# A gated decoder on one core: the conditional expert blocks behind everything, and the last attention head turned by TensorE

## The chip, the cores and the metric

The kernel runs on one core of one Trainium2 chip. The core has five engines with a queue of instructions each: TensorE (PE in the profile; its weight loads are PEld), VectorE (DVE), ScalarE (ACT), GpSimd (POOL) and SyncE (SP), which issues most DMAs. An engine takes its own instructions in order and waits on semaphores for the others. The metric is the device time of one execution in microseconds (us), as the median of several runs.

## The reference

Four layers are added to x (4 sequences of 512 tokens, 512 wide), each with a gate tanh(g). Each layer works on the layer norm of x.

```python
x = x + tanh(g_xattn[0]) * L0_xattn(layernorm(x), ctx, ...)   # x mixed by softmax(q k^T), d = 128
x = x + tanh(g_ffn[0])   * L0_ffn(layernorm(x), ...)          # a 512x512 linear with weights from bits
x = x + tanh(g_xattn[1]) * L1_xattn(layernorm(x), ctx, ...)   # 16 heads of 128, q and k normed
x = x + tanh(g_ffn[1])   * L1_ffn(layernorm(x), ...)          # 16 experts of 352, top 4
```

The third layer, per sequence and head:

```python
q = rmsnorm(h @ Wq, gq); k = rmsnorm(ctx @ Wk, gk); v = ctx @ Wv
attn = softmax(q @ k.T * 128 ** -0.5)
out = concat_heads(attn @ v) @ Wo
```

The fourth layer, for the tokens of the first sequence (the table of choices covers 512 tokens):

```python
out[token] += weight * (silu(xs @ gate[e].T) * (xs @ up[e].T)) @ down[e].T   # for each of 4 chosen e
```

## The kernel before

Everything is float32. A 128x512 float32 matmul is two passes in the trace, so its records come in pairs. x stays in SBUF as x_sb, one tile of 128 tokens by 512 for each of 16 token blocks.

**Stages.** The first layer, then the linear layer and the routing (`route`) run first; the first score matmul of the third layer starts at 211 us. The rest is the third layer with the expert blocks of the fourth spread through it. There are 32 groups m (4 sequences by 8 pairs of heads), and 64 heads i = 2m + h. The work is written out by hand as 64 steps of one head each, and two more; a step has four quarters, one for each chunk of 128 queries. `step(i)` lists what each quarter holds, `put` adds the expert work and the layer norms, and inside `manual_schedule` each engine gets its instructions in the order in which they are written. `later(n, f)` puts f off until a counter, which `tick` advances with the matmuls, has moved on by n.

**One head.** `scores(i, c)` multiplies a chunk of 128 queries with 512 keys into psS (L709). DVE takes the maximum (L717, L719), ACT the exponential with its row sum (L722), DVE the reciprocal and the scaling (L726, L727). The probabilities must be turned so that keys lie on the partitions. `turn_probs` (L243) transposes blocks of 32 by 32 on DVE into tP, and after the fourth chunk `move_probs` (L251) puts the blocks in place with 16 DMAs on SP's queue (tP to big). Two steps later `values(i)` multiplies v with them into psO (L749), ACT copies the result to oT (L756), and `project(m, chunks)` multiplies oT with Wo into psA (L776); DVE adds it to x_sb (L258). After the last group of a sequence the rows of x_sb go out (L771). In even steps the keys and values of the next group are made (L586), in odd steps its queries (L660). The keys are normed, turned on DVE and written to DRAM and read back by DMAs from ACT's queue (L630, L638).

**Psum.** Tags and buffers: psA 3, psS 2, psT 2, psO 1. A matmul into a buffer waits until the reader of what lay there is done.

**Experts.** Each expert takes up to 128 tokens as one slot; slots 16 and up are for experts with more. Slot 16 and the 16 regular ones are always worked, one in two steps, from step 22 (`block_work`): rows are gathered (`load_rows`), transposed (L845), multiplied (L853, L881), and the result goes to the table y_d in DRAM (`keep_rows`, L890). Step 56 is the last of them (`last`). At its end `count_over` loads the number of extra slots into a register of every engine (L932).

**The conditional.** Between step 56 and step 57 stands `further(17)` (L894): if more than one extra slot is in use, it works slot 17, and in it, nested, all further ones up to 30. With the inputs here the number is 1, so every engine skips the body. [...] the skip path of each engine waits for that engine's own earlier work and adds the difference.

Then steps 57 to 60 fetch four rows of y_d each per token from POOL's queue (`add_row`, L915) and add them to x_sb, weighted, and the remaining heads follow. Steps 64 and 65 hold only the values of heads 62 and 63 and their projections.

Of the kernel before, what the change touches and what calls it, by code (L numbers as in the profile page):

```python
# [15 lines left out]
P = 128  # L16
NB = 4
S = 512
DM = 512
# [35 lines left out]
def tile_gated_decoder(  # L55
# [31 lines left out]
    def ps_a():  # L87
        return ps("psA", 3)
# [443 lines left out]
    turned, moved = {}, {}  # L532

    def cols(m):
        g = groups[m][1]
# [19 lines left out]


    clock, pending, serial = [0], [], iter(range(1 << 30))
    quiet = [False]

    def later(n, f):  # L560
        heapq.heappush(pending, (clock[0] + n, next(serial), f))

    def tick(n=1):
        if n == 0:
            return
        clock[0] += n
        while pending and pending[0][0] <= clock[0]:
            heapq.heappop(pending)[2]()
# [135 lines left out]
    def scores(i, c):  # L704


        m, h = divmod(i, G)
        sc = ps_s()
        nc.tensor.matmul(  # L709
            sc, q_of[m][h][:, c * P : (c + 1) * P], k_of[m][:, :, h, :], start=True, stop=True  # L710
        )
# [24 lines left out]
        tick()  # L736
        later(0, top)
        later(2, share)
        later(3, turn)

    def values(i):
# [18 lines left out]

        later(0, copy)

    def project(m, chunks):

        b, g = groups[m]
        oT, wo = o_of[m], wo_of[m]

        def add(t, pp):
            add_to_x(t, pp, tg[:, 1:2])
            if g == NG - 1 and b > 0:  # L770
                nc.sync.dma_start(out_v[:, t, :], x_sb[:, t, :])  # L771

        for c in chunks:
            pp = ps_a()
            for j in range(G):
                nc.tensor.matmul(  # L776
                    pp, oT[:, j, c * P : (c + 1) * P], wo[:, j, :], start=(j == 0), stop=(j == G - 1)
                )
                tick()
            later(1, lambda t=b * NC + c, pp=pp: add(t, pp))  # L780
# [68 lines left out]
    def hidden(st, a):  # L849

        st[a] = ps_a()
        for k in range(KC):
            nc.tensor.matmul(  # L853
                st[a][:, :FF], st["xgT"][:, k * P : (k + 1) * P], st["gu"][:, a, k, :],
                start=(k == 0), stop=(k == KC - 1),
            )
            tick(0 if quiet[0] else 0.7)


    def gate(st):  # L860
# [17 lines left out]
    def down(st):  # L878
        st["py"] = ps_a()
        for f, (_, n) in enumerate(FCH):  # L880
# [4 lines left out]
            tick(0 if quiet[0] else 1)  # L885

    def keep_rows(s, st):
        y = row("y", 2)
        nc.vector.tensor_copy(y, st["py"])
        nc.sync.dma_start(y_d[s * P : (s + 1) * P, :], y)  # L890

    def further(s):

        with tc.If(n_over[0] > s - NE):  # L894
            quiet[0] = True
            load_hidden(s)
            load_down(s)
            load_rows(s)
# [5 lines left out]
            gated(st)  # L904
            hidden_T(st)
            down(st)
            keep_rows(s, st)
            quiet[0] = False
            if s + 1 < NSLOT:
                further(s + 1)  # L910

    def add_row(c, k):

        yg = row("y", 2)
        nc.gpsimd.indirect_dma_start(  # L915
            out=yg,
            out_offset=None,
            in_=y_d[:, :],
            in_offset=bass.IndirectOffsetOnAxis(ap=posi[:, k, c : c + 1], axis=0),
        )  # L920

        def add():
            add_to_x(c, yg, tw[:, c * TOPK + k : c * TOPK + k + 1])
# [10 lines left out]
    def block_work(s, then):  # L934
# [8 lines left out]
            (1, 2): [lambda: down(st()), lambda: later(1, lambda: keep_rows(s, st()))],  # L943
        }
        if then is not None:
            work_of[0, 3] = [lambda: load_hidden(then)]
# [79 lines left out]
    def step(i):  # L1026
        m, h = divmod(i, G)
        pieces = [[], [], [], []]
        if i >= G:
            pieces[2].append(lambda: values(i - G))  # L1030
        elif h > 0:
            pieces[3].append(lambda: tick(8))
        if h == 0:
            if 0 < m < M - 1:
                pieces[0].append(lambda: keys_values(m + 1, [0, 1]))
# [7 lines left out]
        else:  # L1043
            if m + 1 < M:
                pieces[0].append(lambda: queries(m + 1, 0))
                pieces[1].append(lambda: queries(m + 1, 1))
# [85 lines left out]
```

## Time and profile before

Three runs took 1504.64, 1505.93 and 1507.05 us. The profiled execution took 1506.07; its span, from the first instruction to the last, is 1504.3.

| | us |
|---|---|
| median of 3 runs | 1505.93 |
| profiled execution | 1506.07 |
| its span | 1504.3 |
| PE busy (with PEld beside it: 671.2) | 1440.6 |
| DVE busy | 961.6 |
| ACT busy | 522.1 |
| POOL busy | 287.4 |
| the 16 DMA engines, share held by SP's and ACT's queues | 40.8% and 7.3% of the span |

A row of the costliest groups names line, engine, operation, tiles out<-in, shape and count; then the busy time and the mean of one in ns; then the idle time of the engine just before these instructions and what ended most of it. Matmuls are pipelined, so the mean of one is latency; what one costs in a row of them is the distance from start to start. A row in order of time has start, duration, engine, line, tiles and count, and in brackets the idle time before it with its releaser. A row of stretches has the stretch, its length, the busy time (and count) of PE, PEld, DVE, ACT and POOL, the granted PE clock (1.00 is full), the share of the DMA engines and GB/s.

### The profile page before, as it was taken

To read this page: it belongs to the slowest core of one execution; us is meant where nothing else is said; L and a number is where in the kernel's file an instruction comes from. 1 tells how busy PE (TensorE), PEld (TensorE's weight loads), DVE (VectorE), ACT (ScalarE), POOL (GpSimd) and SP (SyncE) were. 2 spreads that over 40 slices of the span, in tenths; PEclk is the share of its full clock that TensorE was granted. 3 is DMA by queue.
4 is the path that set the end of the run, shared out by engine and by line. 5 is a ranking of instruction groups with operands and counts; after the bars stand their busy time and mean duration, and the time that the engine had idled before them with its cause. 6 is when DMAs were issued, how large, how long until landed. Compare 5 with 4: busy or idle time off the path is not lost. (4 is left out here: it accounts for less than half of the span.)

```text
span 1504.3 us, 13711 instructions
## 1 busy us (share of the span) xinstructions
PE 1440.6 (96%) x3705; PEld 671.2 (45%) x3705; DVE 961.6 (64%) x2170; ACT 522.1 (35%) x1175; POOL 287.4 (19%) x210
## 2 busy tenths in 40 slices
PE   5899999899999999999999999999999999989987
PEld 2444444344444444444444444444444444434433
DVE  5875537577777777666565655566656655666783
ACT  3521224333343433333333333324333333333331
POOL 2434411221111111111101111112011111112210
PEclk8899999999999999999999999999999999999998
DMA  9610013554444546456665665556656655545643
GB/s 332 231 47 1 15 56 84 151 145 135 126 143 135 147 137 178 117 170 193 174 185 171 184 203 155 174 163 201 184 164 184 184 169 177 171 121 156 182 126 91
DMA packets 156114, 227.93 MB, mean 152 GB/s; under 512 B 24832, under 2 KB 90896, under 8 KB 156032
## 3 DMA queue, kind: packets, MB, share of 16 engines
q1 hardware_dynamic: 128080, 178.91, 40.8%
q10 hardware_dynamic: 23040, 33.56, 7.3%
q0 software_dynamic: 4912, 14.53, 3.4%
q8 instruction: 32, 0.52, 0.1%
q14 instruction: 50, 0.41, 0.1%
HBM read 129.62 MB, written 30.17 MB: 106 GB/s over the span
## 5 line engine op out<-in xcount | busy, mean ns | idle before, releaser
L722 ACT ACTIVATE prob<-psS,sb,rq 128x512 f32<-128x512 f32 x256 | 199.2, 778 | 605.3 <-DVE sb L719 582.0
L709 PE MATMUL psS<-kT,qT 128*128 128x512 f32 x512 | 263.1, 597 | 4.5 <-DMA big<-tP 2.5
L776 PE MATMUL psA<-wo,oT 128*128 128x512 f32 x512 | 238.6, 604 | 11.7 <-ACT oT L756 11.7
L660 PE MATMUL psA<-lnT,wq 128*128 128x512 f32 x512 | 232.9, 596 | 8.2 <-DVEq L894 7.6
L749 PE MATMUL psO<-big,v 128*128 128x512 f32 x512 | 232.8, 598 | 5.2 <-DMA big<-tP 5.2
L586 PE MATMUL psA<-wkv,ctx 128*128 128x512 f32 x512 | 233.5, 596 | 0.2 <-DVE x_sb L258 0.2
L717 DVE TENSOR_REDUCE nmax<-psS 128x1 f32<-128x512 f32 x256 | 173.0, 676 | 39.5 <-PE psS L709 37.6
L243 DVE STREAM_TRANSPOSE tP<-prob 128x512 f32<-128x512 f32 x256 | 181.9, 711 | 9.0 <-DVE prob L727 0.6
L726 DVE RECIPROCAL rden<-den 128x1 f32<-128x1 f32 x256 | 40.6, 159 | 224.6 <-ACT prob L722 219.0
L749 PEld LDWEIGHTS psO<-big,v 128*128 128x128 f32 x512 | 98.1, 192 | 129.6 <-issue 121.7
L776 PEld LDWEIGHTS psA<-wo,oT 128*128 128x128 f32 x512 | 96.9, 193 | 131.0 <-issue 105.4
L660 PEld LDWEIGHTS psA<-lnT,wq 128*128 128x128 f32 x512 | 97.2, 191 | 129.6 <-issue 107.6
L173 POOL TENSOR_TENSOR rq<-qss,mhalf 128x8 f32<-128x8 f32 x32 | 53.3, 1667 | 516.6 <-DVE qss L696 516.6
L258 DVE SCALAR_TENSOR_TENSOR x_sb<-psA,tg,x_sb 128x512 f32<-128x512 f32 x160 | 113.8, 728 | 57.6 <-PE psA L776 21.8
L586 PEld LDWEIGHTS psA<-wkv,ctx 128*128 128x128 f32 x512 | 96.8, 191 | 118.8 <-issue 106.5
L727 DVE TENSOR_SCALAR prob<-prob,rden 128x512 f32<-128x512 f32 x256 | 133.5, 521 | 9.0
L173 POOL TENSOR_TENSOR rk<-kss,mhalf 128x8 f32<-128x8 f32 x32 | 52.5, 1640 | 447.5 <-DVE rden L726 279.8
L709 PEld LDWEIGHTS psS<-kT,qT 128*128 128x128 f32 x512 | 93.2, 191 | 95.6 <-issue 73.2
L853 PE MATMUL psA<-gu,xgT 128*128 128x352 f32 x272 | 86.0, 459 | 0.0
L623 DVE STREAM_TRANSPOSE tK<-kn 128x256 f32<-128x256 f32 x128 | 45.5, 413 | 49.5 <-POOL kn L612 49.5
L853 PEld LDWEIGHTS psA<-gu,xgT 128*128 128x128 f32 x272 | 51.7, 190 | 37.9 <-issue 16.3
L756 ACT COPY oT<-psO 128x512 f32<-128x512 f32 x64 | 37.4, 585 | 77.4 <-PE psO L749 70.2
(157 smaller groups left out, 1283.7 us busy)
## 6 DMA issues: line engine op xcount, KB each, us to landing
big<-tP SPq DMA_DIRECT2D x1024, 64.0 KB
wq<-in_wq_dram SPq DMA_DIRECT2D x32, 512.0 KB
wo<-in_wo_dram SPq DMA_DIRECT2D x32, 512.0 KB
k_d<-tK ACTq DMA_DIRECT2D x32, 512.0 KB
kT<-k_d ACTq DMA_DIRECT2D x128, 128.0 KB
gu<-in_gate_dram SPq DMA_DIRECT2D x16, 704.0 KB
gu<-in_up_dram SPq DMA_DIRECT2D x16, 704.0 KB
wkv<-in_wk_dram SPq DMA_DIRECT2D x32, 256.0 KB
```

Of the source, the lines that this page charges most:

```text
L173: nc.gpsimd.tensor_tensor(out, v, mhalf[:, :n], ALU.pow)
L243: nc.vector.transpose(tP[:, :, c, :], e.rearrange("p (j r) -> p j r", r=TB))
L258: nc.vector.scalar_tensor_tensor(x_sb[:, t, :], src, gate, x_sb[:, t, :], ALU.mult, ALU.add)
L586: nc.tensor.matmul(pp, ctxs[b][:, k, c * P : (c + 1) * P], wkv[:, k, :, :].rearrange("p a n -> p (a n)"), start=(k == 0), stop=(k == CC - 1),)
L660: nc.tensor.matmul(pp, wq[:, k, h * D : (h + 1) * D], lx1[b][:, k, :], start=(k == 0), stop=(k == KC - 1))
L709: nc.tensor.matmul(sc, q_of[m][h][:, c * P : (c + 1) * P], k_of[m][:, :, h, :], start=True, stop=True)
L717: nc.vector.tensor_reduce(nmax, sc, AX.X, ALU.max, negate=True)
L722: nc.scalar.activation(st["e"], sc, AF.Exp, bias=sb, scale=scale, accum_out=st["den"])
L727: nc.vector.tensor_scalar(st["e"], st["e"], rden, None, ALU.mult)
L749: nc.tensor.matmul(po, v[:, k, h * D : (h + 1) * D], pT[:, :, k, :], start=(k == 0), stop=(k == NC - 1))
L776: nc.tensor.matmul(pp, oT[:, j, c * P : (c + 1) * P], wo[:, j, :], start=(j == 0), stop=(j == G - 1))
L853: nc.tensor.matmul(st[a][:, :FF], st["xgT"][:, k * P : (k + 1) * P], st["gu"][:, a, k, :], start=(k == 0), stop=(k == KC - 1),)
```

## The change

1. The conditional blocks leave their place between steps 56 and 57. All steps now stand in one stretch, and a new function `spill` follows them. In its body, which runs if more than one extra slot is in use, a second table more_d is filled with zeros, `further(17)` writes its slots there, and 16 gathers add the rows to x_sb once more and store the first sequence's rows again. `add_row` keeps reading y_d, where slots 17 to 30 are zero.
2. `project` takes psA, psO, psT and psA for chunks 0, 1, 2 and 3, in every group.
3. The last head (63) has no 32x32 transposes and no moves. Its exponential writes the columns in another order; `end_turn(c)` transposes four 128x128 pieces of chunk c on PE and copies them (DVE for even c, ACT for odd), and `end_values(c)` multiplies v with the 128 queries of that chunk and copies them to oT.
4. Step 63 is the last. It holds values(61) in its first quarter, the projection of group 30 in quarters 2 and 3, and in the last quarter values(62), the pieces of head 63 and the projection of group 31 chunk by chunk. Steps 64 and 65 are gone.

In the built program the last output store stands on SP behind the conditional; the three before it stand ahead of it. The load of wo at the end of step 56 stands behind the moves of head 56, not ahead of them.

```diff
@@ route and tables
+    more_d = dram.tile([NSLOT * P, DM], F32, name="more_d")
...
@@ scores
-            nc.scalar.activation(st["e"], sc, AF.Exp, bias=sb, scale=scale, accum_out=st["den"])
+            e, x = st["e"], sc
+            if i == n_heads - 1:
+                e = e.rearrange("p (k t r) -> p k t r", k=NC, r=TB)
+                x = sc.rearrange("p (t k r) -> p k t r", t=NT, r=TB)
+            nc.scalar.activation(e, x, AF.Exp, bias=sb, scale=scale, accum_out=st["den"])
...
         def turn():
+            if i == n_heads - 1:
+                ends[c] = st["e"]
+                return
...
+    def end_turn(c):
+        if c == 0:
+            ends["pT"] = big()
+        e, pt = ends.pop(c), ps_t()
+        for k in range(NC):
+            nc.tensor.transpose(pt[:, k * P : (k + 1) * P], e[:, k * P : (k + 1) * P], ident)
+        tick(0.5)
+        dst = ends["pT"][:, :, c * P : (c + 1) * P]
+        copy = nc.scalar.copy if c % 2 else nc.vector.tensor_copy
+        later(0, lambda: copy(dst, pt.rearrange("p (k q) -> p k q", k=NC)))
+
+    def end_values(c):
+        m, h = divmod(n_heads - 1, G)
+        po = ps_a()
+        for k in range(NC):
+            nc.tensor.matmul(
+                po[:, 0:P], v_of[m][:, k, h * D : (h + 1) * D],
+                ends["pT"][:, k, c * P : (c + 1) * P], start=(k == 0), stop=(k == NC - 1),
+            )
+        tick(1)
+        later(0, lambda: nc.scalar.copy(o_of[m][:, h, c * P : (c + 1) * P], po[:, 0:P]))
...
@@ project
-            pp = ps_a()
+            pp = (ps_a, ps_o, ps_t, ps_a)[c]()
...
+    def spill():
+
+        with tc.If(n_over[0] > SPILL):
+            zero = row("xgT", 1)
+            nc.vector.memset(zero, 0.0)
+            nc.sync.dma_start(
+                more_d.rearrange("(s p) d -> p s d", p=P),
+                zero.unsqueeze(1).broadcast_to([P, NSLOT, DM]),
+            )
+            further(NE + SPILL)
+            for c in range(NC):
+                for k in range(TOPK):
+                    add_to_x(c, rows_of(more_d, c, k), tw[:, c * TOPK + k : c * TOPK + k + 1])
+                nc.sync.dma_start(out_v[:, c, :], x_sb[:, c, :])
...
@@ step
         if i >= G:
-            pieces[2].append(lambda: values(i - G))
+            pieces[0 if i == n - 1 else 2].append(lambda: values(i - G))
...
+        if i == n - 1:
+            pieces[1].append(lambda: project(m - 1, [0, 1]))
+            pieces[2] += [lambda: project(m - 1, [2, 3]), lambda: end_turn(0)]
+            pieces[3] += [lambda: values(i - 1), lambda: end_turn(1)]
+            pieces[3] += [lambda: end_values(0), lambda: end_turn(2), lambda: end_values(1)]
+            pieces[3] += [lambda: project(m, [0]), lambda: end_turn(3), lambda: end_values(2)]
+            pieces[3] += [lambda: project(m, [1]), lambda: end_values(3)]
+            pieces[3] += [lambda: project(m, [2]), lambda: project(m, [3])]
...
     with tc.manual_schedule():
-        for i in range(last + 1):
-            step(i)
-    further(NE + SPILL)
-    with tc.manual_schedule():
-        for i in range(last + 1, n + G):
+        for i in range(n):
             step(i)
         tick(20)
+    spill()
```

More of the change, by code (lines that the diff above doesn't have):

```diff
@@ L531, in tile_gated_decoder @@
     q_of, sq_of, rq_of, kn_of, k_of, v_of, o_of = {}, {}, {}, {}, {}, {}, {}
-    turned, moved = {}, {}
+    turned, moved, ends = {}, {}, {}
+    n_heads = G * len(groups)
     def cols(m):
@@ L557, in tile_gated_decoder @@
     clock, pending, serial = [0], [], iter(range(1 << 30))
-    quiet = [False]
     def later(n, f):
@@ L563, in tick @@
     def tick(n=1):
-        if n == 0:
-            return
         clock[0] += n
@@ L856, in hidden @@
             )
-            tick(0 if quiet[0] else 0.7)
+            tick(0.7)
     def gate(st):
@@ L884, in down, with keep_rows @@
             )
-            tick(0 if quiet[0] else 1)
-    def keep_rows(s, st):
+            tick()
+    def keep_rows(s, st, table):
         y = row("y", 2)
         nc.vector.tensor_copy(y, st["py"])
-        nc.sync.dma_start(y_d[s * P : (s + 1) * P, :], y)
+        nc.sync.dma_start(table[s * P : (s + 1) * P, :], y)
     def further(s):
         with tc.If(n_over[0] > s - NE):
-            quiet[0] = True
             load_hidden(s)
@@ L906, in further, with rows_of @@
             down(st)
-            keep_rows(s, st)
-            quiet[0] = False
+            keep_rows(s, st, more_d)
             if s + 1 < NSLOT:
                 further(s + 1)
-    def add_row(c, k):
+    def spill():
[11 more added lines that the diff above has]
+                nc.sync.dma_start(out_v[:, c, :], x_sb[:, c, :])
+    def rows_of(table, c, k):
         yg = row("y", 2)
@@ L917, in add_row @@
             out_offset=None,
-            in_=y_d[:, :],
+            in_=table[:, :],
             in_offset=bass.IndirectOffsetOnAxis(ap=posi[:, k, c : c + 1], axis=0),
         )
+        return yg
+    def add_row(c, k):
+        yg = rows_of(y_d, c, k)
         def add():
@@ L942, in block_work @@
             (1, 0): [lambda: hidden_T(st())],
-            (1, 2): [lambda: down(st()), lambda: later(1, lambda: keep_rows(s, st()))],
+            (1, 2): [lambda: down(st()), lambda: later(1, lambda: keep_rows(s, st(), y_d))],
         }
@@ L1042, in step @@
                 pieces[3].append(lambda: later(4, lambda: load_wo(m)))
-        else:
+        elif i < n - 1:
             if m + 1 < M:
```

## The prediction

> **What bounds the kernel now.** I read the page's first part, then its costliest groups, then TensorE (PE) in order of time in the last 165 us, then that stretch with all engines. Times below are us from the span's start.
>
> ```profile
> span 1504.3 us, 13711 instructions
> PE 1440.6 (96%) x3705; PEld 671.2 (45%) x3705; DVE 961.6 (64%) x2170; ACT 522.1 (35%) x1175; POOL 287.4 (19%) x210
> ...
> L776 PE MATMUL psA<-wo,oT 128*128 128x512 f32 x512 | 238.6, 604 | 11.7 <-ACT oT L756 11.7
> L660 PE MATMUL psA<-lnT,wq 128*128 128x512 f32 x512 | 232.9, 596 | 8.2 <-DVEq L894 7.6
> L749 PE MATMUL psO<-big,v 128*128 128x512 f32 x512 | 232.8, 598 | 5.2 <-DMA big<-tP 5.2
> ```
>
> PE is the bound: 96% busy, 63.7 us idle in the whole span, and in the middle steps nearly nothing to gain: between 570 and 1345 the order of time shows no idle worth a mark before any PE group. A change in the tail is therefore worth the PE idle that it removes and the PE work that it adds. Two idle stretches lie where the change works. L894 is the conditional: 7.6 us before L660. L749 waits 5.2 us for the moved probabilities of the last head.
>
> ```profile
> 1347.38 1.02 PE L709 MATMUL psS<-kT,qT 128*128 128x512 f32 x2
> 1356.00 5.33 PE L660 MATMUL psA<-lnT,wq 128*128 128x512 f32 x8 [7.60 <-DVEq L894]
> 1361.16 1.02 PE L709 MATMUL psS<-kT,qT 128*128 128x512 f32 x2
> 1362.02 3.60 PE L660 MATMUL psA<-lnT,wq 128*128 128x512 f32 x8
> ...
> 1408.81 1.13 PE L776 MATMUL psA<-wo,oT 128*128 128x512 f32 x2 [2.63 <-ACT oT L756]
> ...
> 1446.86 1.12 PE L776 MATMUL psA<-wo,oT 128*128 128x512 f32 x2 [1.80 <-ACT oT L756]
> ...
> 1463.23 1.88 PE L709 MATMUL psS<-kT,qT 128*128 128x512 f32 x4
> 1466.41 1.12 PE L709 MATMUL psS<-kT,qT 128*128 128x512 f32 x2 [1.30 <-DMA big<-tP]
> ...
> 1487.33 6.20 PE L749 MATMUL psO<-big,v 128*128 128x512 f32 x8 [5.21 <-DMA big<-tP]
> 1493.37 7.11 PE L776 MATMUL psA<-wo,oT 128*128 128x512 f32 x16
> ```
>
> Columns: start, duration, engine, line, tiles, count, idle before and its releaser. The reader is to see three things. The same eight matmuls take 5.33 after the 7.60 idle and 3.60 six us later; after the 5.21 idle they take 6.20. And the granted clock, by stretches (start:end, length, PE, PEld, DVE, ACT, POOL busy, then the clock), says why:
>
> ```profile
> 1356.00:1361.00 5.00, 5.00 (x8) 2.27 (x9) 0.00 (x0) 0.00 (x0) 0.00 (x0) 0.67 0.45 112
> 1361.00:1400.00 39.00, 39.00 (x93) 17.32 (x92) 28.72 (x60) 14.55 (x33) 13.09 (x11) 1.00 0.53 146
> ...
> 1448.00:1450.00 2.00, 2.00 (x5) 0.97 (x5) 0.99 (x4) 0.87 (x2) 0.00 (x0) 0.51 0.48 182
> ```
>
> So a pause costs its length and then matmuls at half clock. The last row follows an idle of only 1.80 us, while the 2.63 idle at 1408.81 was followed by a full clock: a short pause may or may not cost it.
>
> **Part 1, the conditional leaves step 57.** Its body doesn't run: 4 gathers of gate weights and 17 y_d stores are those of the 17 unconditional slots. What stalls PE is L660: its psum buffer would have been last read inside the body, so it waits for a DVE count that the skip path gives only when DVE reaches the branch, after all its softmax work (branch at 1355.3). POOL's row gathers likewise wait for SP's skip path (1363.0). Without it PE goes on at 1348.4, when the score matmul before ends. Gain: 7.60 idle + (5.33 - 3.60) slow restart = 9.3. The register load of the count stays (0.5 to 0.9 us on each engine's queue); PE's was done at 1342.3 while matmuls were queued, so nothing. On SP the wo load now goes behind sixteen probability moves and that register load, some 14 us later (1347.6 to about 1361.5); its reader, project of the group, comes at 1405, so nothing.
>
> What the pause covered: ACT and DVE caught up in it. In the next two steps with the same work, PE then waits for ACT's oT copy (2.63, 1.80), since ACT stood at the key reloads (L638). I walked step 57 without the pause: PE reaches project's second matmul at 1348.4 + 3.43 + 0.86 + 3.43 + 0.86 + 3.43 + 0.86 + 0.86 = 1362.1; ACT's oT copy ends at about 1361.8 if the four key reloads take some 2 us (0.80 + 0.93 at 1363.2), and at about 1363.9 if 4 us, as at 1402.4. So 0 to 2.6 of new idle, and up to 1.7 of half clock behind it: from 0 to 4.3. I take 1.0, near the quick reload. Net 8.3.
>
> **Part 2, project's psum.** Chunks 1 and 2 of every project move from psA (3 buffers) to psO (1) and psT (2). The PE work is the same. The next user of psO, values, comes two quarters later: for the project chunk that ends near 1411.7 the add (about 0.7) is done by 1415, values starts at 1421.6. psT's next users come some 15 us later. Covered by more than 5 us of other matmuls in each of the 32 groups; relief of psA is worth at most the 0.2 idle at L586. Nothing.
>
> **Part 3, the last heads.** Let S be the start of the first score matmul of head 63 (1463.23). Before: PE ends at 1500.48, S + 37.25. Its work there is four scores (0.86 each), values of 61, 62, 63 (3.43 each) and sixteen 128x512 project matmuls (0.86 each): 3.44 + 10.3 + 13.7 = 27.5. The rest is 1.30 + 5.21 idle, 2.6 half clock (6.20 - 3.60) and overlaps.
>
> Removed: sixteen moves on SP (10.2 us from 1475.28, then some 2 to land), the four DVE 32x32 transposes (0.7 each), one ACT copy. Added on PE: 16 transposes and 32 passes of 128 columns in place of 8 of 512. The pitch is read from starts:
>
> ```profile
> 821.09 0.60 PE L845 MATMUL psT<-ident,xg 128*128 128x128 f32 x4
> 821.53 1.02 PE L709 MATMUL psS<-kT,qT 128*128 128x512 f32 x2
> ```
>
> Four transposes: 0.44, so 1.76 in all. A 512-column pass has a pitch of 0.43, 128 columns 0.107, so 32 of them 3.44, as much as values(63) before. PE work after: 3.44 + 6.86 + 13.7 + 1.76 + 3.44 = 29.2.
>
> [...] The trace's mean for L845 is also 273 ns, but that is latency; the pitch is 0.11. [...] I take the row; the clock stayed 1.00 through step after step with such transposes. Each group of four lies between other matmuls here too.
>
> Does PE find its operands? From S: scores 0.86, values(61) to 4.3 (its moves, the first sixteen of the 32 SP issues from 1451.50, land near 1464.3, S + 1.0: at most 0.4 late), project of group 30 and three scores to 12.9, first transposes to 13.3. DVE then has the psum copy (0.7), one add (0.7), the last chunk's maximum, ACT's exponential and the scaling: probabilities of chunk 3 at S + 17.5. PE meanwhile does the last score and values(62) (moves landed by S + 12.2, read from 14.2), to 17.6, then transposes and chunked values of 0 and 1 to 20.3, project chunk 0 to 22.0, and needs chunk 3 only there. ACT copies chunk 1 by 19.0 (read at 19.4) and each oT piece 0.5 after its values; its reader comes 0.86 later or more. PE ends at S + 29.3: 8.0 earlier.
>
> Then the end. The last add and store follow as before (add 1500.52 to 1501.27, store at 1501.3, landed by 1503.0, end 1504.3), but the fourth output store now stands behind the conditional on SP, whose skip path waits for every store to land. The third store lands 1.75 after issue (as the last one before); five more semaphore events at 0.06 and the branch, about 0.4: the fourth store leaves 2.15 after the third, where a project chunk's 1.72 would have set it. Cost 0.45; with the branch's whole 1.44 (1362.0 to the next load at 1363.44) 1.5. [...] The rows: 0.5 from SP's branch to its next event; PE's branch alone shows 3.47. At SP's row the cost is 0.45, at PE's about 3.5. PE's own branch at the end (3.47 after S + 29.3) is covered by the add, the store and its landing. I take 0.5.
>
> Part 3: 8.0 - 0.5 - 0.4 (moves of 61) = 7.1. The rearranged exponential writes pieces of 32; the oT copy with pieces of 32 took 585 ns beside 582 for a plain psum copy, so nothing.
>
> **Sum.** 8.3 + 7.1 = 15.4 against the profiled execution of 1506.07 (span 1504.3 and 1.8 around it): 1490.7. The median of the three runs is 0.14 lower, so 1490.5.
>
> **Rivals.** (a) The pause is given back: steps 57 to 61 wait for ACT, with half clocks behind: 4.3 at 57 and one more of 3; the gain is 9 and the time 1497. For it: the 2.63 and 1.80 rows; against: in the steps of the same shape before the experts' work began (280 to 600) PE had two such waits, 0.49 and 1.58. (b) The last head is latency-bound: [...] 128-column passes held by their weight loads of 0.19 (32 x 0.083 = +2.7), SP's branch at 3.5 (+3): part 3 gives nothing, 1498. (c) Slower: psO, single, makes values wait for the DVE add of project chunk 1 in every group. It needs 15.4 / 31 = 0.50 us in each group to break even and 0.6 to be slower; at the 1 us of an add behind a late softmax, 1521. Against it the 5 us of cover. (d) The conditional costs PE no time by itself, some other late engine holds step 57 as long, and the tail gains nothing: no change, 1506.
>
> **How the numbers follow.** What a measurement here tells from no change is about 0.2%, 3 us. Both gains as worked out 0.74 (1490.5); (a) 0.12 (1497); (b) 0.08 (1498); (c) 0.04 (1521); (d) 0.02. Faster 0.94, same 0.02, slower 0.04. Range: below, no new wait (1.0), no late moves (0.4) and the half clock of 1448 gone (1.7): 1487.4; above, (a) and (b): 1498.
>
> **What would show it.** Right: no L894 row before L660; PE ends about 29 us after the first score of head 63; no idle over 1 us before the last chunked values; clock 1.00 to the end; the fourth store about 2.2 behind the third. Wrong: idle before project's second matmul of step 57 above 2.6; idle before values marked DVE x_sb; transposes that start more than 0.15 apart.

## The result, and the profile after

The kernel before took 1506.49 us (median of 6 runs beside the changed kernel, 1504.64 to 1509.28), the changed kernel 1495.53 us (median of 6, 1492.66 to 1497.79). The ratio is 0.9922, 95% interval 0.9905 to 0.9940: 11.0 us faster by the medians, where 15.4 were predicted. The time lies within the range given, 5.0 us above the predicted 1490.5.

The profiled execution of the changed kernel took 1497.79 us, the slowest of its six, with a span of 1495.9, so it shows less of the gain than the medians do. The page's first part and its costliest groups:

```profile
span 1495.9 us, 13741 instructions
PE 1439.1 (96%) x3745; PEld 675.5 (45%) x3745; DVE 963.7 (64%) x2168; ACT 523.3 (35%) x1180; POOL 286.7 (19%) x210
...
L659 PE MATMUL psA<-lnT,wq 128*128 128x512 f32 x512 | 231.1, 592 | 0.5 <-DMA wq<-in_wq_dram 0.5
L755 PE MATMUL psO<-big,v 128*128 128x512 f32 x504 | 227.3, 594 | 0.0
...
L806 PE MATMUL psA<-wo,oT 128*128 128x512 f32 x256 | 123.8, 602 | 12.0 <-ACT oT L762 12.0
```

The query matmuls (now L659) no longer wait for the conditional (7.6 us before, now 0.5 for weights), and the values (now L755) no longer wait for moved probabilities (5.2 before, now 0.0). The project step (now L806) waits for ScalarE's output copy as it did, 12.0 against 11.7. TensorE in order of time:

```profile
1348.86 1.02 PE L708 MATMUL psS<-kT,qT 128*128 128x512 f32 x2
1349.71 3.60 PE L659 MATMUL psA<-lnT,wq 128*128 128x512 f32 x8
...
1393.05 1.12 PE L708 MATMUL psS<-kT,qT 128*128 128x512 f32 x2 [0.89 <-DMA big<-tP]
...
1402.53 2.07 PE L806 MATMUL psA<-wo,oT 128*128 128x512 f32 x2 [3.21 <-ACT oT L762]
...
1442.06 1.12 PE L806 MATMUL psA<-wo,oT 128*128 128x512 f32 x2 [1.77 <-ACT oT L762]
...
1449.63 2.07 PE L708 MATMUL psS<-kT,qT 128*128 128x512 f32 x2 [2.79 <-DMA big<-tP]
1451.50 4.28 PE L755 MATMUL psO<-big,v 128*128 128x512 f32 x8
...
1459.91 1.02 PE L708 MATMUL psS<-kT,qT 128*128 128x512 f32 x2
...
1472.79 0.60 PE L776 MATMUL psT<-ident,prob 128*128 128x128 f32 x4
1473.22 1.02 PE L708 MATMUL psS<-kT,qT 128*128 128x512 f32 x2
...
1487.55 1.88 PE L806 MATMUL psA<-wo,oT 128*128 128x512 f32 x4
```

The pause is gone: the query matmuls of step 57 follow their score at once and take 3.60. But in steps 59 to 62 TensorE stands for 0.89, 3.21, 1.77 and 2.79 us, 8.7 in all, where the kernel before stood for 6.25 (0.62, 2.63, 1.80, 1.20). Twice the granted clock is then 0.50 (1402.0 to 1405.0 and 1449.6 to 1452.0): behind 3.21 and 2.79 two matmuls take 2.07, where behind 1.77 they take 1.12. By stretches, columns as in the prediction, both of these and the tail:

```profile
1402.00:1409.00 7.00, 6.47 (x10) 3.12 (x11) 5.81 (x15) 1.35 (x4) 2.62 (x2) 0.54 0.79 262
1449.00:1452.00 3.00, 2.37 (x3) 1.17 (x4) 1.34 (x5) 1.37 (x4) 0.00 (x0) 0.58 0.46 112
1452.00:1490.00 38.00, 37.43 (x122) 19.01 (x120) 20.01 (x42) 9.11 (x21) 0.00 (x0) 0.99 0.27 78
```

From head 63's first score (1459.91) TensorE works without a gap and ends at 1489.43, 29.5 later. Then the end. The instructions of the conditional, with their durations in ns and their starts (q marks the engine's queue):

```profile
L942 SPq EVENT_SEMAPHORE  x8: 17/17/17, 1491.9 to 1492.4; - x8
...
L942 ACTq COMPARE_BRANCH  x1: 45/45/45, 1486.0 to 1486.0; - x1
...
L942 ACTq EVENT_SEMAPHORE  x1: 17/17/17, 1486.5 to 1486.5; - x1
L942 SPq COMPARE_BRANCH  x1: 50/50/50, 1488.9 to 1488.9; - x1
```

SyncE compares at 1488.9, and its next instruction runs only at 1491.9. Its eight events are its skip path: in the trace each waits on a semaphore and adds to it, and three of the semaphores are those of the first three stores. The fourth output store stands behind that and leaves at 1492.6, though its data were ready at 1490.2 (the last addition, 1489.47 and 0.75). From the start of that addition to the end of the span are 6.43 us, where the kernel before had 3.78.

So the pair of spans differs by 8.4 us: 4.8 gained between the score ahead of step 57 and head 63's first score (115.85 before, 111.05 after), 7.7 in the tail, 2.65 lost at the end, and 1.5 lost ahead of step 57. That last is there at the first scores already (211.00 and 213.00), before any changed work; other runs start them between 210.7 and 214.0.

### The profile page after: what moved, and what is told of

It reads as the page before. It is cut to its first block, busy times and chain, and to the rows that moved or that the text cites. A ratio compares the mean times of both kernels' runs of the same rounds, so it can differ in the third digit from the quotient of the medians.

```text
span 1495.9 us, 13741 instructions
## 1 busy us (share of the span) xinstructions
PE 1439.1 (96%) x3745; PEld 675.5 (45%) x3745; DVE 963.7 (64%) x2168; ACT 523.3 (35%) x1180; POOL 286.7 (19%) x210
## 4 chain that ended last, share of the span: by engine, by line
PE 78%; DVE 7%; SPq 4%; ACT 3%; DMA 3%; issue 3%; POOL 2%; ACTq 0%; POOLq 0%; DVEq 0%
PE psA L585 13%; PE psS L708 12%; PE psO L755 11%; PE psA L659 11%; PE psA L806 6%; PE psA L883 5%; PE psO L806 4%; SPq L251 3%; PE psT L806 3%; PE psA L911 3%; PE psA L287 3%; PE psA L512 3%; DMA big<-tP 2%; ACT prob L725 2%; DMA x_sb<-in_x_dram 1%
## 5 line engine op out<-in xcount | busy, mean ns | idle before, releaser
L659 PE MATMUL psA<-lnT,wq 128*128 128x512 f32 x512 | 231.1, 592 | 0.5 <-DMA wq<-in_wq_dram 0.5
L755 PE MATMUL psO<-big,v 128*128 128x512 f32 x504 | 227.3, 594 | 0.0
L659 PEld LDWEIGHTS psA<-lnT,wq 128*128 128x128 f32 x512 | 96.7, 190 | 120.4 <-issue 108.8
L755 PEld LDWEIGHTS psO<-big,v 128*128 128x128 f32 x504 | 96.2, 191 | 121.5 <-issue 114.0
L806 PE MATMUL psA<-wo,oT 128*128 128x512 f32 x256 | 123.8, 602 | 12.0 <-ACT oT L762 12.0
L258 DVE SCALAR_TENSOR_TENSOR x_sb<-psA,tg,x_sb 128x512 f32<-128x512 f32 x96 | 70.0, 729 | 39.2 <-PE psA L512 21.7
L806 PEld LDWEIGHTS psA<-wo,oT 128*128 128x128 f32 x256 | 48.5, 192 | 74.9 <-issue 55.9
L806 PE MATMUL psO<-wo,oT 128*128 128x512 f32 x128 | 64.6, 629 | 0.0
```

The source lines that it names most:

```text
L258: nc.vector.scalar_tensor_tensor(x_sb[:, t, :], src, gate, x_sb[:, t, :], ALU.mult, ALU.add)
L659: nc.tensor.matmul(pp, wq[:, k, h * D : (h + 1) * D], lx1[b][:, k, :], start=(k == 0), stop=(k == KC - 1))
L755: nc.tensor.matmul(po, v[:, k, h * D : (h + 1) * D], pT[:, :, k, :], start=(k == 0), stop=(k == NC - 1))
L806: nc.tensor.matmul(pp, oT[:, j, c * P : (c + 1) * P], wo[:, j, :], start=(j == 0), stop=(j == G - 1))
```

## The experiments

Three questions: what the end costs, what each part gives alone, and where the gain between steps 57 and 62 went. "The end" below is the time from the start of VectorE's last addition to the end of the span: 3.78 us before, 6.43 in the changed kernel. "The stretch" runs from the score ahead of step 57 to head 63's first score: 115.85 and 111.05.

A single execution does not fix the stretch. Up to head 63, five of the kernels run the same code: the changed kernel and the first four variants below. Their stretches took 111.05, 111.16, 111.27, 108.42 and 109.11 us, in that order.

### The end without the conditional

```diff
         tick(20)
-    spill()
```

> The changed kernel without the conditional behind everything. It leaves out the conditional itself: with these inputs its body is not entered, so nothing else of the work is missing. Theory F (the taken branch is slow [...], 3.0 us on SyncE, and the fourth output store is issued behind it): the fourth store follows the last addition to x by about 0.4 us instead of 2.4, and the time from TensorE's last matmul to the end of the span falls from 6.5 us to 3.8, as in the kernel before; 2.6 us less in all, a ratio to the kernel before of about 0.990. Rival N (the end is longer for another reason, such as the store's own landing or a slow queue): the stretch stays above 5.5 us and the ratio stays at 0.992. Everything ahead of head 63 should stand as in the changed kernel by either.

Measured: ratio 0.9888 (0.9868 to 0.9908). The fourth store leaves 0.8 us after the last addition starts (3.1 in the changed kernel), as theory F said. The end is 5.1 us and not 3.8; one of the last four stores took 3.2 us to land here and the median 2.0, which fits the difference. The 2.3 us of the store's delay go with the conditional: in the changed kernel SyncE's branch (3.0 us to its first event) and its eight events (0.5) stand ahead of that store.

### All stores ahead of it

```diff
         tick(20)
-    spill()
+        spill()
```

> The changed kernel with the conditional taken into the region whose order is written out by hand, so that all four output stores stand ahead of it on SyncE. Theory F: the fourth store leaves about 0.4 us after the last addition and lands 2.2 us later, so it no longer sets the end; but each engine still takes its branch behind its last work, TensorE's for 3.5 to 3.8 us, and the program ends only behind it: 4.2 to 5.2 us from TensorE's last matmul to the end of the span (6.5 in the changed kernel, 3.8 before), 1.3 to 2.3 us gained. Rival W (SyncE's 3.0 us are a wait for the other engines' parts of the conditional[...]): the stretch is governed by the same exchange, and SyncE's branch shrinks to the 0.5 us that it took in the kernel before, since the store is no longer between; the stretch falls to 3.8 to 4.2 us.

Measured: ratio 0.9921 (0.9902 to 0.9940), the end 6.29 us. Nothing is gained, and both theories missed. The conditional's instructions:

```profile
L942 SPq EVENT_SEMAPHORE  x8: 17/17/17, 1495.1 to 1495.6; - x8
...
L942 DVEq COMPARE_BRANCH  x1: 72/72/72, 1491.0 to 1491.0; - x1
...
L942 SPq COMPARE_BRANCH  x1: 50/50/50, 1492.2 to 1492.2; - x1
L942 DVEq EVENT_SEMAPHORE  x1: 21/21/21, 1494.0 to 1494.0; - x1
```

The store left at 1491.8, but SyncE's branch now starts behind it, still takes 2.9, and the program's closing steps stand behind the branch. The same 3 us lie on the path, only in another order: SyncE must both issue the last store and take the branch. Rival W falls: the branch is as long with no store behind it.

### The skipping path laid next

```diff
-        with tc.If(n_over[0] > SPILL):
+        with tc.If(n_over[0] > SPILL, preferred_fallthrough_block=False):
```

> The changed kernel with the blocks of the conditional laid out otherwise: the path that skips the body comes next behind the compare, and the jump over the body stands behind that path as an unconditional one. Theory F (jumping far is what costs): the compare is over in some 0.5 us, the semaphore events follow at once, and then the jump costs its 3.0 us, still ahead of the fourth store; the stretch from TensorE's last matmul to the end stays at 6 to 6.8 us and nothing is gained. Rival C (a compare costs, by its register or its wait, and a plain jump whose target is known does not): the fourth store leaves 2 to 2.5 us earlier and the stretch falls to about 4 us, ratio about 0.990.

Measured: ratio 0.9923 (0.9899 to 0.9947), the end 8.4 us.

```profile
L942 SPq EVENT_SEMAPHORE  x8: 17/17/17, 1486.6 to 1488.4; - x8
...
L942 SPq COMPARE_BRANCH  x2: 41/47/53, 1486.5 to 1488.4; - x2
```
```profile
1491.12 0.33 SPq L801 DMA_DIRECT2D out_dram<-x_sb  x1
```

The compare at 1486.5 is followed by the first event 0.1 us later. The jump at 1488.4 is followed by the store's wait only at 1491.0, 2.6 us later. So the jump costs here and the compare does not, and rival C falls. The end was longer than F gave, because the events now come one after the other with a wait of 1.4 us among them (the last runs at 1488.4, 2.3 us after the third store left at 1486.1), and the jump begins behind them.

### A short body

The stores ahead of the conditional as above, and:

```diff
-            further(NE + SPILL)
             for c in range(NC):
-                for k in range(TOPK):
-                    add_to_x(c, rows_of(more_d, c, k), tw[:, c * TOPK + k : c * TOPK + k + 1])
                 nc.sync.dma_start(out_v[:, c, :], x_sb[:, c, :])
```

> As the kernel whose four stores stand ahead of the conditional, but with a body of one clearing, one write of a table and four stores; it leaves out the overflowing expert blocks and their additions, which these inputs don't enter. TensorE and ScalarE then have no branch at all, and SyncE's jump passes over some ten instructions. Theory F with distance [...]: SyncE's branch takes about 0.5 us, and the stretch from TensorE's last matmul to the end is 3.8 to 4.2 us. Rival T (any taken branch costs the same, near or far): SyncE's and VectorE's branches take 2.9 to 3.5 us as before, and the stretch is 4.2 to 5.2 us.

Measured: ratio 0.9893 (0.9870 to 0.9916), the end 4.07 us.

```profile
L942 SPq EVENT_SEMAPHORE  x5: 17/17/17, 1488.9 to 1489.2; - x5
...
L942 DVEq COMPARE_BRANCH  x1: 72/72/72, 1487.5 to 1487.5; - x1
L942 DVEq EVENT_SEMAPHORE  x1: 21/21/21, 1488.3 to 1488.3; - x1
L942 SPq COMPARE_BRANCH  x1: 50/50/50, 1488.7 to 1488.7; - x1
```

SyncE's branch takes 0.2 us. VectorE's event comes 0.8 after its compare, which is the addition itself (0.75). So the taken branch over the short body is nearly free in this run, and this short conditional costs 0.3 us at the end: rival T falls. (TensorE and ScalarE do have a branch here, of 223 and 45 ns, well before the end.)

### Part 1 alone

The conditional and its table as in the changed kernel, the last head and the project step's PSUM tags as before:

```diff
...
-            pp = (ps_a, ps_o, ps_t, ps_a)[c]()
+            pp = ps_a()
...
-        for i in range(n):
+        for i in range(n + G):
             step(i)
         tick(20)
     spill()
```

> Part 1 alone: the conditional stands behind everything as in the changed kernel, with its own table; the last head goes by the 32-square moves and the project step has one PSUM tag, as before. Theory L (the pause of 7.6 us is gone, some 4.5 us of it are lost again to waits on ScalarE in steps 59 to 62, and SyncE's far branch costs 2.6 at the end): TensorE's stretch from the score ahead of step 57 to the first score of head 63 takes about 111 us (115.85 before), TensorE's last matmul to the end 6 to 6.5 us, together 2 to 3 us faster, ratio 0.998 to 0.9985. The prediction's account (8.3 gained, 0.5 at the end): the stretch takes 107.5 us, ratio 0.995. Rival (the loss in steps 59 to 62 comes of the new PSUM tags or of the new tail): the stretch takes 107 to 108.5 us here, ratio near 0.997.

Measured: ratio 0.9966 (0.9954 to 0.9979), 5.1 us faster. The stretch takes 108.9, between theory L's 111 and the prediction's 107.5, and within what the five kernels with the changed kernel's code took. The end is 6.26, as theory L had it.

```profile
1400.10 1.12 PE L800 MATMUL psA<-wo,oT 128*128 128x512 f32 x2 [3.08 <-ACT oT L756]
...
1438.68 1.12 PE L800 MATMUL psA<-wo,oT 128*128 128x512 f32 x2 [2.32 <-ACT oT L756]
1439.78 3.60 PE L800 MATMUL psA<-wo,oT 128*128 128x512 f32 x4
```

The waits of steps 59 to 62 are there without the new tags and the new tail. Whether they come with the pause's going, the next run shows. Here the 3.08 us were not followed by half pace (1.12 for two matmuls and then 1.96 for four), and the 2.32 were (1.12, then 3.60 for four).

### Parts 2 and 3 alone

```diff
...
-            keep_rows(s, st, more_d)
+            keep_rows(s, st, y_d)
...
-        for i in range(n):
+        for i in range(last + 1):
             step(i)
+    further(NE + SPILL)
+    with tc.manual_schedule():
+        for i in range(last + 1, n):
+            step(i)
         tick(20)
-    spill()
```

> Parts 2 and 3 alone: the last head's probabilities by TensorE and the project step's PSUM tags as in the changed kernel, and the conditional in its old place ahead of step 57 with its writes going to the old table. Theory L: from head 63's first score TensorE ends 29.3 to 29.7 us later (37.25 before) and the end holds no branch, so 3.8 to 4.5 us from TensorE's last matmul to the end; 7 to 8 us faster, ratio 0.995. The pause ahead of the query matmuls of step 57 is still there with 7 to 8 us, since a branch in that place has the same waits behind it. Rival (the two parts overlap: the tail gains only because the conditional has left the middle): under 5 us, ratio above 0.9965. On SyncE the branch in the middle should take 0.5 us as in the kernel before if its price hangs on the place, and near 3 us if it hangs on the length of the body alone.

Measured: ratio 0.9958 (0.9941 to 0.9974), 6.3 us faster. The pause is back, and SyncE's and VectorE's branches take half a microsecond in the middle, over the same long body:

```profile
1354.76 6.63 PE L663 MATMUL psA<-lnT,wq 128*128 128x512 f32 x8 [7.64 <-DVEq L928]
```
```profile
L928 SPq EVENT_SEMAPHORE  x8: 17/17/17, 1361.2 to 1361.8; - x8
...
L928 SPq COMPARE_BRANCH  x1: 50/50/50, 1360.7 to 1360.7; - x1
```

From head 63's first score (1466.73) TensorE ends 29.5 later, and the end takes 3.81 us. So the tail gives its 7.7 us by itself. The two parts add up: 5.1 and 6.3 are 11.4, against 11.8 for the whole (0.0078 of 1507). Length alone did not make the branch slow, since this one passes over the long body in 0.5.

The waits of steps 59 to 62 stand here too, behind the pause:

```profile
1409.56 2.07 PE L810 MATMUL psA<-wo,oT 128*128 128x512 f32 x2 [3.31 <-ACT oT L766]
...
1456.43 2.07 PE L712 MATMUL psS<-kT,qT 128*128 128x512 f32 x2 [2.79 <-DMA big<-tP]
```

With the 1.63 between them they are 7.7 us, and the stretch takes 120.6, where the kernel before, with the same pause, had 6.25 and 115.85. So these waits do not come with the pause's going.

### Part 2 alone, and part 2 only where the tail needs it

```diff
-            pp = ps_a()
+            pp = (ps_a, ps_o, ps_t, ps_a)[c]()
```

> Part 2 alone: the kernel before with the project step's four accumulators from psA, psO, psT and psA again, where it had psA for all. Theory of the prediction: nothing, within 0.1% (0.999 to 1.001), since the step's matmuls were not waiting for a psA buffer. Rival (one psO and one psT buffer make values and the sum over parts wait for the project step's addition): 2 to 15 us slower, ratio 1.0015 to 1.010. Rival (part of the gain of the whole is from here): ratio 0.997 to 0.9985, with the wait of the project step's second matmul group on ScalarE's copy shorter than 2.6 us.

Measured: ratio 1.0009 (1.0001 to 1.0017, 20 runs), 1.4 us slower if anything. The wait for the output copy is not shorter: 3.27 us where it was 2.63. Its profiled execution has a pause of 7.65, then waits of 7.8 in steps 59 to 62 and a stretch of 120.8.

```diff
-            pp = (ps_a, ps_o, ps_t, ps_a)[c]()
+            pp = ((ps_a, ps_o, ps_t, ps_a)[c] if m >= len(groups) - 2 else ps_a)()
```

> The changed kernel with the project step's four accumulators all from psA, as before, and the change of tags only for the last two pairs of heads, which the reordered end needs. Theory P (part 2 costs some 1.4 us along the whole kernel, the 1.0009 measured for it alone): 1.4 us faster than the changed kernel, ratio about 0.991. Rival (what was measured for part 2 alone hangs on the old end [...]): no difference, ratio 0.992.

Measured: ratio 0.9925 (0.9911 to 0.9940), no faster than the changed kernel. Taking the tags out of the other groups gives nothing back. So part 2 gains nothing, and whether it costs 1 us or so is open.

### The keys by another queue

```diff
-                nc.scalar.dma_start(
+                (nc.gpsimd if m >= 29 else nc.scalar).dma_start(
                     kT[j * TB : (j + 1) * TB].rearrange("r t h q -> r t (h q)"),
```

> The changed kernel with the four transfers that bring the turned keys back (kT) issued from GpSimd's queue for the last three pairs of heads and not from ScalarE's. Theory K (ScalarE stands at the third of these transfers for 2.9 us at 1397 because its issue waits for transfers of SyncE that share its completion semaphore, and the squares, queries, exponential and output copy behind it are late): the idle time of TensorE ahead of the project step's matmul near 1402 falls from 3.2 to under 1.2 us, and with it the half clock behind it goes; 3 to 5 us faster than the changed kernel, ratio about 0.989 to 0.990. Rival V (VectorE is what is late there, loaded with the additions of the fourth layer's rows): the idle time stays at 2.5 us or more, and the ratio at 0.992. Rival Q (GpSimd's queue takes longer to issue and land them, and the keys come late instead): a new wait of the scores for kT, ratio above 0.993.

This came from ScalarE and VectorE in the changed kernel ahead of the 3.21 us wait:

```profile
1388.10 10.75 SPq L251 DMA_DIRECT2D big<-tP  x16
...
1394.38 0.71 DVE L258 SCALAR_TENSOR_TENSOR x_sb<-y,tw,x_sb 128x512 f32<-128x512 f32 x1
...
1396.10 0.98 ACTq L637 DMA_DIRECT2D kT<-k_d  x2
...
1397.12 2.90 ACTq L637 DMA_DIRECT2D kT<-k_d  x2
...
1400.07 0.60 ACT L665 ACTIVATE sq<-psA 128x512 f32<-128x512 f32 x1 [3.28 <-DMA big<-tP]
...
1401.89 0.59 ACT L762 COPY oT<-psO 128x512 f32<-128x512 f32 x1
```

ScalarE's third key transfer goes out at 1397.1 and the fourth only at 1399.7: in the trace its issue waits on the semaphore of one of SyncE's moves, which was issued at 1395.7 and landed at 1399.7. The squares, the exponential and the output copy queue behind it.

Measured with GpSimd's queue: ratio 0.9912 (0.9895 to 0.9928). The stretch takes 105.6 us, and the wait is 1.73 with full pace behind it (1.13 for two matmuls, then 1.96 for four). No score waits for keys. Theory K is right in direction but explains about half of the wait. The gain over the changed kernel, some 1.5 us by the ratios, is within their intervals.

### Without the fourth layer's additions

```diff
-            put(last + 1 + c, k, lambda c=c, k=k: add_row(c, k))
+            pass
```

> The changed kernel without the fourth layer's gathers of expert rows and their additions to x, 16 of each with 0.74 us on VectorE an addition; it leaves that part of the output out. Rival V (the waits of steps 59 to 62 come from VectorE being late with these additions): TensorE's idle time near 1402 falls under 1 us and the stretch from the score ahead of step 57 to head 63's first score goes from 111 to below 107, ratio about 0.989. Theory K (ScalarE is held by its key transfers, which share completion semaphores with SyncE's moves): the idle time near 1402 stays at 2.5 us or more, ratio 0.991 to 0.992.

Measured: ratio 0.9837 (0.9821 to 0.9853), 12.8 us faster than the changed kernel, and the stretch falls to 98.6 us. TensorE, where it waited 3.21 and 2.79:

```profile
1394.59 1.88 PE L806 MATMUL psA<-wo,oT 128*128 128x512 f32 x4
...
1436.25 1.12 PE L708 MATMUL psS<-kT,qT 128*128 128x512 f32 x2 [1.57 <-ACT prob L725]
```

and the queues, with the key transfers still on ScalarE's:

```profile
1382.33 10.43 SPq L251 DMA_DIRECT2D big<-tP  x16
...
1385.67 0.35 ACTq L629 DMA_DIRECT2D k_d<-tK  x1
...
1389.82 1.80 ACTq L637 DMA_DIRECT2D kT<-k_d  x3
```

One wait of 1.57 is left, and no half clock (1.00 from 1346 to 1445). Counted from the score ahead of step 57, SyncE's sixteen moves start at 36.0 here and at 39.2 in the changed kernel, and the keys are put out at 39.4 and at 43.3. Five of the additions, 3.6 us, stand ahead of those moves on VectorE in the changed kernel, and VectorE never stood idle for a gathered row (the last column, of the changed kernel):

```profile
L258 DVE SCALAR_TENSOR_TENSOR x_sb<-y,tw,x_sb 128x512 f32<-128x512 f32 x16 | 11.5, 717 | 0.0
```

So rival V holds, and it holds the other theory within it: VectorE's additions make the softmax and the key transposes late, hence the moves, hence the key transfers that wait for them, hence ScalarE and TensorE. But the run also leaves out the gathers' traffic. Over the stretch the DMA engines moved 161 GB/s in the changed kernel (1349 to 1460), where a move took 2.9 us from issue to landing at the median (1355 to 1450), and 128 GB/s here (1346 to 1445). What that adds, behind the late start of the moves, was not separated.

This run is also a ruler: its stretch takes 98.6 with neither pause nor additions. The kernel before took 17.2 more: pause 7.60, slow restart 1.73, idle 6.25 less the 1.57 that remain without additions, half clock 1.7, together 15.7. The changed kernel took 12.4 more: idle 8.66 less 1.57, and half clock 4.5 (the pieces behind 1402.53 and 1449.63 at 2.07, 3.76, 2.07 and 4.28 where full speed is 1.12, 1.88, 1.12 and 3.60), together 11.6.

Did the pause cover part of the additions? What the stretch has above the ruler, less the pause and its slow restart:

| | us | idle in steps 59 to 62 |
|---|---|---|
| with the pause: before | 7.9 | 6.4 |
| with the pause: parts 2 and 3 alone, part 2 alone | 11.3, 11.4 | 7.7, 7.8 |
| without it: part 1 alone | 10.3 | 8.1 |
| without it: the five kernels with the changed kernel's code | 9.8 to 12.6 | 7.3 to 9.2 |

The pair alone (7.9 and 12.4) would say that the pause covered 4.5 us; the other rows do not bear it out. The idle time differs by about 1 us between the means with the pause and without it. Part of the rest goes with the half clock (1.7 us of it in the kernel before, 4.5 in the changed one).

### The better version

```diff
...
-                nc.sync.dma_start(out_v[:, t, :], x_sb[:, t, :])
+                q = nc.scalar if m == len(groups) - 1 and c == NC - 1 else nc.sync
+                q.dma_start(out_v[:, t, :], x_sb[:, t, :])
...
-    spill()
+        spill()
```

with the keys on GpSimd's queue as above.

> The changed kernel with the key transfers of the last three pairs on GpSimd's queue, the conditional in the ordered region, and the fourth output store on ScalarE's queue, whose own branch took 0.5 us in the changed kernel. SyncE then takes its branch behind the third store, beside VectorE's last addition. Theory F with this: from the start of VectorE's last addition to the end 4.8 to 5.4 us (6.4 in the changed kernel), together with the keys 2.5 to 5 us faster, ratio 0.989 to 0.9905. Rival (VectorE's own far branch of 2.9 us, behind the last addition, then sets the end): 5.8 to 6.4 us, ratio 0.991.

Measured: 1491.71 us, ratio 0.9890 (0.9873 to 0.9906), the fastest of the kernels that do the whole work, against 0.9922 for the changed kernel; the two intervals just touch. The end takes 6.29 us, so the gain is not from there:

```profile
L943 SPq EVENT_SEMAPHORE  x8: 17/17/17, 1488.4 to 1488.9; - x8
...
L943 SPq COMPARE_BRANCH  x1: 50/50/50, 1483.8 to 1483.8; - x1
L943 DVEq COMPARE_BRANCH  x1: 72/72/72, 1484.3 to 1484.3; - x1
...
L943 DVEq EVENT_SEMAPHORE  x1: 21/21/21, 1487.2 to 1487.2; - x1
```

SyncE compares 4.6 us before its first event; with the keys alone moved the two were 2.9 apart (1483.8 and 1486.7). The event comes 3.3 us after ScalarE's store left at 1485.1; that it waited for that store to land is my reading of it. The rival's time is right, but VectorE's event at 1487.2 was not the last.

> The one before with the change of PSUM tags kept to the last two pairs of heads too. If the three gains add: 4 to 6 us faster than the changed kernel, ratio 0.988 to 0.9895. If the waits of steps 59 to 62 have one limit in common behind them: as the one before, 0.989 to 0.991.

With the PSUM line of the run on part 2 added: 1493.71 us, ratio 0.9906 (0.9891 to 0.9921). No further gain shows, as in the run on part 2.

## Why the prediction was right or wrong

| step of the sum | predicted | the profiled pair |
|---|---|---|
| part 1: pause and slow restart, less new waits | 8.3 | 4.8 |
| part 3: TensorE from head 63's first score to its end, less late moves | 7.6 | 7.7 |
| the end, with the far branch | -0.5 | -2.65 |
| ahead of step 57 | 0 | -1.5 |
| sum | 15.4 | 8.4 (medians: 11.0) |

The last column is one execution of each kernel, the changed one's the slowest of six. The medians' 11.0 (9.0 to 14.3 by the ratio's interval) are 4.4 below the sum. The end explains 2.15 of that; the other 2.3 lie within the interval. The kernel without the conditional agrees: by its ratio it gains 16.9 us (13.9 to 19.9), and the sum without its term for the end is 15.9.

**The pause: right.** It was the skip path's count from VectorE (its event at 1355.92, the matmuls at 1356.00), it went with the conditional, and the eight matmuls ran in 3.60. The walk through step 57 held too: project's second matmul (1362.59 and 1364.45) finds its copy without a wait.

**"What the pause covered": wrong in place and cause, and its size not refuted.** I saw the 2.63 and 1.80 us waits, put them down to ScalarE standing at the key reloads, and looked for a new one in step 57 alone. None came there. The waits stand one and two groups later, with the pause and without it. The cause that I named is the last link of a chain; at its head stand VectorE's sixteen additions with their gathers, which the run without them shows: 98.6 against 111.05 us. I took 1.0 us for the new waits. The profiled pair has 9.3 less 4.8, which is 4.5, but the table of the stretches shows that this pair cannot be taken for the kernels. By the medians part 1 alone gained 5.1 us (3.2 to 6.9) although its end cost 2.5, so 7.6 without the end, where 8.3 was predicted. The rival "the pause is given back" leaves 2.0 of the 9.3, and less than nothing once the end is paid, so that run excludes it. That its 1497 lies nearer to the measured 1495.5 than 1490.5 does is luck: it took the end at 0.5 too.

**Part 2: nothing, as predicted,** within about 2 us. The rival in which one psO buffer makes the kernel slower, 1521, is excluded by the 1.0009 (at most 1.0017).

**The tail: right.** TensorE ended at S + 29.5 where S + 29.3 was worked out, with no gap. Four transposes again took 0.43 (1472.79 to 1473.22), not the 1.1 that four times the mean of one in the trace would make (272 ns here, 273 in the kernel before); by an estimate from that mean sixteen would have cost 2.6 more. The clock stayed at 0.99 through them.

**The end: mis-sized, 0.5 for 2.65.** I had two rows of the kernel before, SyncE's branch (0.5 us to its next event) and TensorE's (3.47 us), worked out both, and took SyncE's. At the end of the kernel SyncE's branch took 3.0 us, and the fourth store left 4.0 behind the third where I gave 2.15. The short body's 0.2 us and the jump's 2.6 with the other layout show that the jump over the long body is what costs there. But the length of the jump alone would not have given the number: SyncE's jump over a long body took 0.5 in the middle, in the kernel before and in the one with the new tail alone.

A second term of the same sum was short as well, and the slow branch hid it. In the run without the additions the branch took 0.5 at the end too, and still the fourth store left 3.3 behind the third and the end took 5.9 us:

```profile
L942 SPq EVENT_SEMAPHORE  x8: 17/17/17, 1474.4 to 1476.7; - x8
...
L942 SPq COMPARE_BRANCH  x1: 45/45/45, 1473.9 to 1473.9; - x1
```

SyncE's last event comes there 3.1 us after the third store left, with 1.7 us of waiting among the events, where I had put 1.75 for that store to land. So a cheap branch alone would not have brought the cost down to 0.5.

## What to carry to other kernels

The wait that the bounding engine showed here was only the end of a chain. Take the work that is extra in such steps (here sixteen VectorE additions and their gathers) as the first suspect. Before saying that a stall covered such work, look at the work with the stall and without it in more than one execution of each: the same code took from 108.4 to 111.3 us here, and one pair of profiles told a story that the medians did not bear out.

A conditional whose body is skipped was not free at the very end of this kernel: the end took 6.43 us with it and 5.1 without. Where the last store stood behind it, SyncE first took the branch (0.5 to 3.0 us over the long body) and then went through the skip path's events (the last came 2.3 and 3.1 us after the third store left in two runs). Carry both prices, and both ends of the branch's, into the sum.

## What the hardware showed that was not expected

**A taken branch had several prices.** On SyncE, from the compare to the next event over the long body: 0.5 us in the middle (before, and with the tail alone) and in the run without the additions; 2.9 to 3.0 in the changed kernel, with the stores first, with the keys moved and in part 1 alone. On VectorE at the end, with its 0.75 us addition in between: 0.7 and 0.8 in part 1 alone and without the additions, 2.9 to 3.0 in the others with the long body behind the compare. ScalarE showed 0.4 to 0.6 throughout. What makes a long jump cheap in one program and dear in another is open; no run here varied it by itself.

**How long TensorE stood did not tell whether its clock halved.** Idle times of 3.21 us (changed kernel, granted clock 0.50) and 3.31 (parts 2 and 3 alone) were followed by half pace at once, two matmuls in 2.07 where 1.12 is full pace. 2.97 (the skipping path laid next) and 3.08 (part 1 alone) were not: 1.12, and four more in 1.96. But 1.80 (kernel before, granted clock 0.51), 2.32 (part 1 alone) and 2.37 (the skipping path laid next) were, about 1 us after the matmuls had begun again: 1.12, and four more in 3.66, 3.60 and 3.58.

**A half clock was free once.** From the project matmul near 1442 to the score that waits next it took 7.57 us in the changed kernel (four matmuls in 1.96, then 2.79 idle) and 7.58 with the skipping path laid next (four matmuls in 3.58, then 1.10 idle). In both the score waited for moved probabilities (`<-DMA big<-tP`): these set its time, and TensorE's slower matmuls only filled its wait.
